# Another order of work at the change of batch, in a layer of attention and routed low-rank adapters on one core

## The chip, the core and the metric

The kernel runs on one core of a Trainium2 chip. Five engines of that core work on their own queues, each strictly in the order in which the program was written: PE (matrix products, with its weight loads PEld shown apart), DVE (vector work), ACT (scalar functions and copies), POOL (further vector work) and SP, which issues all DMAs here. Work on one engine that needs a result of another waits on a semaphore, and everything behind it in its queue waits too. The metric is the device time of one execution in microseconds (us); the page and the trace come from one execution that was profiled.

## What is computed

The input x has 4 batches of 1024 rows with 1024 values each, all in float32. Cut to what matters:

```python
x = x + attention(layernorm(x))       # 32 heads of 32 values, rotary q and k, causal, then @ wo
x = x + ffn(layernorm(x))

# attention, per batch
q, k, v = xn @ wq, xn @ wk, xn @ wv
q, k = rotate(q), rotate(k)
probs = softmax(where(causal, q @ k.T / sqrt(32), lowest))
out = (probs @ v) @ wo

# ffn: one of 8 adapters of rank 16 per row
logits = yn @ route_w.T
best, which = top_k(logits, 1)
h = yn @ A.T                          # 8 x 16 values
out = (one_hot(which) * best * h) @ Bw
```

## The kernel before

*Units.* The four heads of one group fill the 128 partitions. A unit is one batch and one group: 4 batches of 8 groups are 32 units. While the scores, the softmax and the value products of unit u run, PE's free time is filled with the projections of unit u+1, and, from batch 1 on, with the output projection, the second layer norm and the adapter of one block of 128 rows of the batch before. The end of a batch is where this text looks: the first projections of the next batch need its rows normalized and transposed, while the last two units of the old batch are still at their scores.

*Rounds.* The eleven entries of SLOTS (line 26) are the rounds of one unit. A score round writes scores of one or more blocks of 64 rows (numbered 0 to 15; "round 12" below is the one that writes block 12) into PSUM. There is one such PSUM tile (`s`, four banks), which the value products (`av`) use too. ACT copies the scores out (L412), POOL adds the causal mask on the diagonal (L415), DVE finds the maxima (L433) and joins those of the two halves (L454), ACT makes the exponentials (L462), DVE transposes them in 32x32 blocks (L487), and PE multiplies them with the values (L568). "first" and "second" apply the value products of blocks 0 to 7 and 8 to 15. After the value products DVE scales the result by the reciprocal sums (L588), and only then is the PSUM tile free.

*Filling.* What PE does between the rounds is a list of steps, `between[u]`, with a cost each. `do_some` takes steps from the list until a round's share of the costs is used up. A step of cost 0 (a load, a fetch, a scaling) goes with the next one that has a cost. Nothing is planned by time: the order of the lists is the order of the queues.

- `chain(u, n, tb)`: eight matmuls of 128x512 that project q, k or v of unit u for the first or the second half of the rows (tb 0 or 1). After the last, ACT copies the result out; for q and k, DVE and POOL rotate it some steps later (L340 to L346). When the second half of one of q, k, v is done, its weights are free and the next weight load is issued; two weight tiles are in rotation.
- `finish_steps(b, t)`: of one block of rows of the finished batch. `fetch` loads its attention and its x; sixteen output matmuls (`po`, L685) follow, whose weights are streamed in chunks; then the second norm. Its four `tail` steps come in the next unit: `turn` (eight transposes of the normalized rows, `pt_f`; one half is copied out by ACT, the other by DVE, L204), `route` (`ph`, L706, and five small DVE steps to the gated hidden values `wh`, L725), `turn_hidden` (`pw`, one transpose) and `adapt` (`pf`, L745, two matmuls, two DVE additions, and the store).
- `Norm` (line 233): the eight blocks of 128 rows ("tiles" 0 to 7) of the next batch. `load` brings tiles in; some land in the tiles that later hold q and k of the next unit (`homes`), the others in one of five row buffers. `find` makes the moments of one tile (two L175, L177, L179 on DVE, then a power on POOL, L181). `scale` applies them (L186 on DVE); before it scales tile k, it finds the moments of tile k+1. `turn` transposes a scaled tile on PE (`pt_a`, L198, two PSUM banks), has ACT copy it into `xnT` (L200, L202), and loads the tiles that `after` names. There are two `xnT` tiles, one for each half of the rows.

*Where the steps of Norm stand.* `change_steps` (line 783) makes the filling of a batch's last unit: the first eight output matmuls mixed with the tail, with the scaling and turning of tiles 2 and 3 and of tile 4, then the chains of the next unit with turns 4 to 7 among them. The first tiles are put into the list of the unit before, by counting places from its end (lines 819 to 837): for batch 0 turns 0 to 3 stand between the last matmuls of that list; from batch 1 on only turn 0 stands there, and turn 1 comes in `change_steps`.

*Buffers.* Apart from the two weight tiles there are five row buffers, four for q and k, two `xnT`, four chunks, one PSUM tile of four banks for scores or value products and four PSUM banks for everything else.

Of the kernel before, what the change touches and what calls it, by code (L numbers as in the profile page):

```python
# [71 lines left out]
def tile_preln_attn_then_top1_lora(  # L72
# [160 lines left out]
    class Norm:  # L233
# [30 lines left out]
        def scale(self, t):  # L264
            while self.scaled <= t:
                k = self.scaled
                self.find(k + 1)
                normalize(self.x[k], self.x[k], self.moments.pop(k))
                self.scaled += 1

        def turn(self, t):
# [8 lines left out]
            self.load(*self.after.get(t, ()))  # L280

# [501 lines left out]
    def change_steps(u, norm, project, tail):  # L783


        p, turning, scaling = project, norm.turning, norm.scaling
# [3 lines left out]
        if p:  # L790
            turn, route, turn_hidden, adapt = tail
            out += [*p[:2], turn, scaling(2), p[2], turning(1), p[3], route, scaling(3), p[4], turning(2)]
            out += [p[5], turn_hidden, p[6], turning(3), adapt, Step(lambda: norm.load(7), 0.0)]
            out += [scaling(4), p[7]]
            chains = weave(chains[:-6], p[8:]) + chains[-6:]
        else:
            out += [scaling(4)]
        for t, n in zip(range(TB, NT), (3, 4, 5, 4)):
            out += chains[:n] + [turning(t)] + [scaling(t + 1)] * (t + 1 < NT)
            del chains[:n]  # L800
        return out + chains
# [4 lines left out]
    for u, (b, g) in enumerate(units):  # L806
        project, new_tail = [], []
        if b:
# [3 lines left out]
            if g:  # L812
                between[-1].insert(max(0, len(between[-1]) - 8), fetch)
# [5 lines left out]
        if u + 1 < len(units) and g + 1 == NG:  # L819
            last_v = between[-1]  # L820
            if b:
                norm = Norm(b + 1, {0: (1,), 1: (4,), 2: (5,), 3: (6,)}, {2: "q", 3: "k", 5: "q", 6: "k"})
                last_v.append(norm.scaling(1))
                last_v.insert(len(last_v) - 9, norm.turning(0))
                last_v.insert(len(last_v) - 18, norm.scaling(0))
                last_v.insert(len(last_v) - 30, Step(lambda norm=norm: norm.load(0), 0.0))
            else:
                norm = Norm(b + 1, {0: (5,), 1: (6,), 2: (7,)})
                for t in reversed(range(TB)):
                    last_v.insert(len(last_v) - 7 + 2 * t, norm.turning(t))  # L830
                for t in (3, 2):
                    last_v.insert(22 * t - 34, norm.scaling(t))
# [3 lines left out]
            steps = change_steps(u + 1, norm, project, tail)  # L836
            norms[b + 1] = norm
        else:
            steps = []
            if u + 1 < len(units):  # L840
                for n, tb in (("q", 0), ("k", 0), ("q", 1), ("k", 1), ("v", 0), ("v", 1)):
                    steps += chain(u + 1, n, tb)
# [261 lines left out]
```

## Time and profile before

| | us |
|---|---|
| median of 3 runs | 2793.89 (2791.73 to 2795.76) |
| the profiled execution | 2790.88 |
| its span, first to last instruction | 2789.1 |
| PE busy | 2699.2 |
| DVE busy | 2132.6 |
| ACT busy | 1753.3 |
| POOL busy | 646.6 |
| mean granted clock of PE | 0.991 |

Busy time is that of the engine's own instructions, without their waits. The granted clock is the share of full speed that PE was given; in a stretch where it is 0.5, PE is as busy as ever and does half the work. The wait table says for each engine and line who released it, with the sum, the number of waits and the longest. Times in an excerpt in order of time count from the start of the span; a bracket behind an instruction tells how long its engine stood idle before it and who ended that. In counts, one matmul of float32 appears as two records. The batches change at about 515 to 570, 1170 to 1255 and 1865 to 1950 us.

### The profile page before, as it was taken

To read this page: it belongs to the slowest core of one execution; us is meant where nothing else is said; L and a number is where in the kernel's file an instruction comes from. 1 tells how busy PE (TensorE), PEld (TensorE's weight loads), DVE (VectorE), ACT (ScalarE), POOL (GpSimd) and SP (SyncE) were. 2 spreads that over 40 slices of the span, in tenths; PEclk is the share of its full clock that TensorE was granted. 3 is DMA by queue.
4 is the path that set the end of the run, shared out by engine and by line. 5 is a ranking of instruction groups with operands and counts; after the bars stand their busy time and mean duration, and the time that the engine had idled before them with its cause. 6 is when DMAs were issued, how large, how long until landed. Compare 5 with 4: busy or idle time off the path is not lost.

```text
span 2789.1 us, 84093 instructions
## 1 busy us (share of the span) xinstructions
PE 2699.2 (97%) x35328; PEld 1329.6 (48%) x35328; DVE 2132.6 (76%) x4201; ACT 1753.3 (63%) x5030; POOL 646.6 (23%) x900
## 2 busy tenths in 40 slices
PE   8999999899999999979999999997999999999998
PEld 5444444444444554444444455443544445544445
DVE  4888889897777778767777777876777777787655
ACT  2877877776666667546666666664676666666421
POOL 2222233232222222222222222221222222222000
PEclk9999999999999999989999999999999999999999
DMA  3222232226444444541654444454265444346421
GB/s 116 51 55 55 62 97 55 66 55 163 142 123 134 115 124 133 154 140 54 170 141 129 130 120 121 128 162 131 59 167 145 123 135 122 118 124 191 129 66 54
DMA packets 448011, 317.86 MB, mean 114 GB/s; under 512 B 150288, under 2 KB 371728, under 8 KB 447632
## 3 DMA queue, kind: packets, MB, share of 16 engines
q1 hardware_dynamic: 447632, 312.47, 40.3%
q8 instruction: 278, 4.55, 0.7%
q14 instruction: 101, 0.83, 0.1%
HBM read 262.59 MB, written 49.81 MB: 112 GB/s over the span
## 4 chain that ended last, share of the span: by engine, by line
PE 83%; DVE 13%; ACT 2%; POOL 1%; issue 1%; DMA 0%; POOLq 0%; SPq 0%; ACTq 0%; DVEq 0%
PE po L685 15%; PE pk L308 14%; PE pq L308 14%; PE pv L308 12%; PE s L401 11%; PE av L568 9%; DVE top L433 4%; DVE pr L487 4%; PE pf L745 2%; PE ph L706 2%; ACT pr L412 1%; PE pr L542 1%; DVE both L454 1%; PE pt_f L198 1%; PE pt_a L198 1%
## 5 line engine op out<-in xcount | busy, mean ns | idle before, releaser
L462 ACT ACTIVATE pr<-pr,both 128x256 f32<-128x256 f32 (+15 forms) x2048 | 1044.9, 519 | 38.9 <-DVE both L454 38.8
L412 ACT COPY pr<-s 128x640 f32<-128x640 f32 (+14 forms) x544 | 525.1, 1017 | 518.1 <-PE s L401 517.5
L433 DVE TENSOR_REDUCE top<-pr 128x2 f32<-128x960 f32 (+15 forms) x768 | 650.9, 894 | 259.0 <-POOL pr L415 258.6
L487 DVE STREAM_TRANSPOSE pr<-pr 128x1024 f32<-128x1024 f32 (+11 forms) x768 | 664.9, 907 | 42.3 <-ACT pr L462 39.0
L415 POOL TENSOR_TENSOR pr<-pr,causal_sb 128x128 f32<-128x128 f32 x512 | 239.7, 474 | 1108.7 <-ACT pr L412 1100.0
L308 PE MATMUL pv<-xnT,wv 128*128 128x512 f32 x1024 | 485.2, 602 | 0.0
L308 PE MATMUL pq<-xnT,wq 128*128 128x512 f32 x1008 | 478.2, 601 | 0.6 <-ACT xnT L200 0.6
L308 PE MATMUL pk<-xnT,wk 128*128 128x512 f32 x1008 | 475.6, 602 | 0.0
L401 PE MATMUL s<-kT,qT 32*32 32x256 f32 (+4 forms) x17408 | 398.1, 390 | 10.9 <-ACT pr L412 4.2
L462 ACT ACTIVATION_READ_ACCUMULATOR pr<-pr,both 128x1 f32 x2048 | 400.7, 196 | 0.0
L685 PE MATMUL po<-chunk,attn 128*128 128x512 f32 x736 | 378.7, 599 | 0.0
L401 PEld LDWEIGHTS s<-kT,qT 32*32 32x32 f32 x17408 | 188.8, 103 | 268.1 <-issue 101.0
L308 PEld LDWEIGHTS pk<-xnT,wk 128*128 128x128 f32 x1008 | 182.6, 190 | 236.7 <-issue 235.4
L308 PEld LDWEIGHTS pv<-xnT,wv 128*128 128x128 f32 x1024 | 186.5, 190 | 218.1 <-issue 213.8
L308 PEld LDWEIGHTS pq<-xnT,wq 128*128 128x128 f32 x1008 | 182.9, 191 | 224.5 <-issue 222.0
L568 PE MATMUL av<-pr,vals 64*32 64x256 f32 (+3 forms) x12288 | 269.8, 318 | 3.6 <-DVE pr L487 3.5
L568 PEld LDWEIGHTS av<-pr,vals 64*32 64x32 f32 x12288 | 212.1, 105 | 111.4 <-issue 36.0
L454 DVE TENSOR_TENSOR both<-top 32x4 f32<-32x4 f32 (+3 forms) x1152 | 216.3, 188 | 23.5
L685 PEld LDWEIGHTS po<-chunk,attn 128*128 128x128 f32 x736 | 135.0, 191 | 163.8 <-issue 153.6
L543 ACT COPY by<-pr 128x512 f32<-128x512 f32 x64 | 37.4, 585 | 266.8 <-PE pr L542 262.8
L588 DVE TENSOR_TENSOR at<-av,by 128x256 f32<-128x256 f32 x128 | 48.1, 417 | 171.1 <-ACT by L543 171.1
L685 PE MATMUL po<-wo,attn 128*128 128x512 f32 x256 | 118.2, 603 | 0.0
(87 smaller groups left out, 1728.8 us busy)
## 6 DMA issues: line engine op xcount, KB each, us to landing
chunk<-in_wo SPq DMA_DIRECT2D x368, 256.0 KB, 3.4
vals<-vd SPq DMA_DIRECT2D x256, 128.0 KB, 4.1
x<-in_x SPq DMA_DIRECT2D x56, 512.0 KB, 4.8
wq<-in_wq SPq DMA_DIRECT2D x32, 512.0 KB, 4.1
wk<-in_wk SPq DMA_DIRECT2D x32, 512.0 KB, 4.1
wv<-in_wv SPq DMA_DIRECT2D x32, 512.0 KB, 4.2
vd<-vT SPq DMA_DIRECT2D x128, 128.0 KB, 4.6
out_y<-x SPq DMA_DIRECT2D x32, 512.0 KB, 2.8
```

The source lines that it names most:

```text
L198: nc.tensor.transpose(pt[:, i, :], src[:, c * P : (c + 1) * P], eye_sb)
L308: nc.tensor.matmul(at["p"], lhsT=wt[:, c, :], rhs=xnTs[b, tb][:, c, :], start=(c == 0), stop=(c == NC - 1),)
L401: nc.tensor.matmul(sc[i * SQ : (i + 1) * SQ, h, at : at + w].rearrange("p (j k) -> p j k", k=SQ), lhsT=of_q[rows, 2 * t + half], rhs=of_k[ ...
L412: nc.scalar.copy(pr[:, :, k0 : k0 + w], sc[:, :, at : at + w])
L415: nc.gpsimd.tensor_tensor(diagonal, diagonal, causal_sb.unsqueeze(1).to_broadcast([P, HG, SQ]), ALU.add)
L433: nc.vector.tensor_reduce(top[:, k, h : h + step], places[u, t][:, h : h + step, :], AX.X, ALU.max, negate=True,)
L454: nc.vector.tensor_tensor(dst[rows], src[rows], src[other], op)
L462: nc.scalar.activation(pr[:, h, :], pr[:, h, :], AF.Exp, bias=tops[u, t][:, h : h + 1], accum_out=dens[u, t // QT][:, t % QT, h : h + 1],)
L487: nc.vector.transpose(pr, pr)
L568: nc.tensor.matmul(avs[half][h * HD : (h + 1) * HD, t0:, :], lhsT=v[rows, j, h * HD : (h + 1) * HD], rhs=rhs, start=(j == 0), stop=(j == n ...
L685: nc.tensor.matmul(st["po"], lhsT=lhsT, rhs=rhs, start=(c == start), stop=(c == stop))
L706: nc.tensor.matmul(ph, lhsT=st["ynT"][:, c, :], rhs=w[:, c - i * RA, :], start=(c == 0), stop=(c == NC - 1),)
```

## The change

No arithmetic is changed. What is changed is where steps stand in the lists, and which tile of the next batch is loaded where.

1. *Order of the last chains.* The unit after which a batch ends projects in the order q0, q1, k0, v0, k1, v1 (the digit is the half of the rows), where all units had q0, k0, q1, k1, v0, v1. So everything that reads the first half of `xnT` is done two chains earlier.
2. *One chain a unit on.* From batch 1 on, the last of these chains, v1, is left out of that list (`held`) and done in `change_steps` of the next, where it takes the place among the tail that the first eight output matmuls had. Those follow later in the same list.
3. *Moments and scaling as steps of their own.* `finding(t)` is a new step. From batch 2 on (`self.b` of the norm over 1), moments of tile k are found in such steps or just ahead of the scaling, and `scale` no longer finds those of k+1. For the norm of batch 1, `scale` finds k+1 after scaling k instead of before it.
4. *Places.* For the norm of batches 2 and 3 the moments, scalings and turns of tiles 0 and 1 and moments and scaling of tile 2 now stand in the list of the unit before, each behind a named chain step. For that of batch 1, turns 0 to 3 stand from the second matmul of k1 on.
5. *Loads.* From batch 2 on tiles 3 and 4 are put into the q and k tiles and later tile 6 into q's (it was 2, 3, 5 and 6), so one tile more uses a row buffer. The fetch for the last unit of a batch stands 3 places from the end of its list instead of 8.

```diff
         def scale(self, t):
             while self.scaled <= t:
                 k = self.scaled
-                self.find(k + 1)
+                self.find(k + 1 if self.b == 0 else k)
                 normalize(self.x[k], self.x[k], self.moments.pop(k))
                 self.scaled += 1
+                if self.b == 1:
+                    self.find(k + 1)
...
+        def finding(self, t):
+            return Step(lambda: self.find(t), 0.0)
...
-    def change_steps(u, norm, project, tail):
+    def change_steps(u, norm, project, tail, held):
...
         if p:
             turn, route, turn_hidden, adapt = tail
-            out += [*p[:2], turn, scaling(2), p[2], turning(1), p[3], route, scaling(3), p[4], turning(2)]
-            out += [p[5], turn_hidden, p[6], turning(3), adapt, Step(lambda: norm.load(7), 0.0)]
-            out += [scaling(4), p[7]]
+            find = norm.finding
+            out += [*h[:2], turn, *h[2:4], turning(2), h[4], find(3), route, h[5], scaling(3), find(4)]
+            out += [h[6], turn_hidden, h[7], p[0], adapt, Step(lambda: norm.load(7), 0.0), scaling(4)]
+            out += [p[1], find(5), p[2], scaling(5), turning(3), p[3], p[4], turning(4), *p[5:8]]
             chains = weave(chains[:-6], p[8:]) + chains[-6:]
-        else:
-            out += [scaling(4)]
-        for t, n in zip(range(TB, NT), (3, 4, 5, 4)):
-            out += chains[:n] + [turning(t)] + [scaling(t + 1)] * (t + 1 < NT)
-            del chains[:n]
-        return out + chains
+            out += [*chains[:2], find(6), *chains[2:4], scaling(6), turning(5), *chains[4:6], find(7)]
+            out += [*chains[6:8], scaling(7), turning(6), *chains[8:14], turning(7)]
+            return out + chains[14:]
+        out += [*chains[:3], scaling(5), turning(4), *chains[3:7], scaling(6), turning(5)]
+        out += [*chains[7:12], scaling(7), turning(6), *chains[12:16], turning(7)]
+        return out + chains[16:]
+
+    USUAL = (("q", 0), ("k", 0), ("q", 1), ("k", 1), ("v", 0), ("v", 1))
+    ENDING = (("q", 0), ("q", 1), ("k", 0), ("v", 0), ("k", 1), ("v", 1))
+
+    def behind(steps, at, step):
+        steps.insert(steps.index(at) + 1, step)
...
-                between[-1].insert(max(0, len(between[-1]) - 8), fetch)
+                apart = 3 if g + 1 == NG and u + 1 < len(units) else 8
+                between[-1].insert(max(0, len(between[-1]) - apart), fetch)
...
             if b:
-                norm = Norm(b + 1, {0: (1,), 1: (4,), 2: (5,), 3: (6,)}, {2: "q", 3: "k", 5: "q", 6: "k"})
-                last_v.append(norm.scaling(1))
-                last_v.insert(len(last_v) - 9, norm.turning(0))
-                last_v.insert(len(last_v) - 18, norm.scaling(0))
-                last_v.insert(len(last_v) - 30, Step(lambda norm=norm: norm.load(0), 0.0))
+                norm = Norm(b + 1, {0: (2,), 2: (5,), 3: (6,)}, {3: "q", 4: "k", 6: "q"})
+                load = [Step(lambda norm=norm, t=t: norm.load(t), 0.0) for t in range(2)]
+                for at, step in (
+                    (own["k", 0][0], load[0]),
+                    (own["v", 0][0], norm.finding(0)),
+                    (own["v", 0][1], load[1]),
+                    (own["v", 0][2], norm.scaling(0)),
+                    (own["v", 0][6], norm.turning(0)),
+                    (own["v", 0][7], norm.finding(1)),
+                    (own["k", 1][0], norm.scaling(1)),
+                    (own["k", 1][3], norm.turning(1)),
+                    (own["k", 1][5], norm.finding(2)),
+                    (own["k", 1][7], norm.scaling(2)),
+                ):
+                    behind(last_v, at, step)
             else:
                 norm = Norm(b + 1, {0: (5,), 1: (6,), 2: (7,)})
-                for t in reversed(range(TB)):
-                    last_v.insert(len(last_v) - 7 + 2 * t, norm.turning(t))
-                for t in (3, 2):
-                    last_v.insert(22 * t - 34, norm.scaling(t))
+                for t, at in enumerate((("k", 1), ("k", 1), ("k", 1), ("v", 1))):
+                    behind(last_v, own[at][(1 + 3 * t) % NC], norm.turning(t))
+                behind(last_v, own["v", 1][5], norm.scaling(4))
+                behind(last_v, own["k", 0][0], norm.scaling(3))
+                behind(last_v, own["q", 0][6], norm.scaling(2))
...
-            steps = change_steps(u + 1, norm, project, tail)
+            steps = change_steps(u + 1, norm, project, tail, held)
...
+            held = []
             if u + 1 < len(units):
-                for n, tb in (("q", 0), ("k", 0), ("q", 1), ("k", 1), ("v", 0), ("v", 1)):
-                    steps += chain(u + 1, n, tb)
+                ends = g + 2 == NG and b + 1 < B
+                own = {}
+                for n, tb in ENDING if ends else USUAL:
+                    own[n, tb] = chain(u + 1, n, tb)
+                    if ends and b and (n, tb) == ("v", 1):
+                        held = own[n, tb]
+                    else:
+                        steps += own[n, tb]
...
             if b:
-                norms[b + 1].load(2, 3)
+                norms[b + 1].load(3, 4)
```

More of the change, by code (lines that the diff above doesn't have):

```diff
@@ L780, in finish_steps @@
         return Step(fetch, 0.0), chains, tail
-    def change_steps(u, norm, project, tail):
-        p, turning, scaling = project, norm.turning, norm.scaling
+    def change_steps(u, norm, project, tail, held):
+        p, h, turning, scaling = project, held, norm.turning, norm.scaling
         out, chains = [], []
```

## The prediction

> **What bounds the kernel now.** First the page: which engine is full, over the whole span.
>
> ```profile
> PE 2699.2 (97%) x35328; PEld 1329.6 (48%) x35328; DVE 2132.6 (76%) x4201; ACT 1753.3 (63%) x5030; POOL 646.6 (23%) x900
> PEclk9999999999999999989999999999999999999999
> ```
>
> PE does nearly all of the span; an order can win only its 90 us of idle time and the time at half clock. Second, the wait table of PE, for who holds it up:
>
> ```profile
> PE pt_a L198 <- DVE x L186: 22.1, 7, 9.2
> PE pt_a L198 <- DVE kT L186: 19.6, 4, 7.4
> PE ph L706 <- DVE yn L204: 8.5, 3, 3.3
> ```
>
> Columns are total us, times, longest. The transposes of the next batch's rows wait for DVE's scaling (L186), and route waits for a DVE copy. Third, windows around the three changes of batch, and one ordinary stretch after the second:
>
> ```profile
> 502.00:570.00 68.00, 58.14 (x1013) 32.42 (x1028) 57.06 (x111) 49.36 (x133) 16.65 (x24) 0.92 0.21 55
> 1153.00:1253.00 100.00, 79.86 (x1062) 43.85 (x1061) 73.94 (x145) 50.00 (x138) 20.00 (x29) 0.92 0.49 143
> 1847.00:1950.00 103.00, 81.03 (x1062) 42.52 (x1061) 74.02 (x145) 50.56 (x140) 19.51 (x29) 0.93 0.47 138
> 1253.00:1353.00 100.00, 100.00 (x1221) 46.42 (x1220) 73.88 (x150) 66.75 (x189) 28.37 (x36) 0.99 0.37 94
> ```
>
> After the length come PE, PEld, DVE, ACT and POOL busy, then the granted clock. The changes cost 9.9, 20.1 and 22.0 us of idle PE, and clocks of 0.92 to 0.93 (8 to 9% of 58 to 81 busy us: 5 to 7 us each): some 70 us in all, the ceiling of any gain. Fourth, the second change in order of time, PE and then DVE:
>
> ```profile
> 1195.06 2.85 PE L706 MATMUL ph<-chunk,yn 128*128 128x136 f32 x16 [3.25 <-DVE yn L204]
> ...
> 1209.92 1.94 PE L198 MATMUL pt_a<-eye_sb,kT 128*128 128x128 f32 x8 [6.05 <-DVE kT L186]
> ...
> 1230.18 1.06 PE L198 MATMUL pt_a<-eye_sb,qT 128*128 128x128 f32 x8 [1.37 <-DVE qT L186]
> ...
> 1240.65 1.94 PE L198 MATMUL pt_a<-eye_sb,kT 128*128 128x128 f32 x8 [3.07 <-DVE kT L186]
> ...
> 1251.06 1.94 PE L198 MATMUL pt_a<-eye_sb,x 128*128 128x128 f32 x8 [3.07 <-DVE x L186]
> ```
>
> ```profile
> 1198.30 0.81 DVE L186 TENSOR_SCALAR qT<-qT,mv_a,rstd_a 128x1024 f32<-128x1024 f32 x1
> ...
> 1199.99 0.29 DVE L725 TENSOR_TENSOR wh<-ph,gate 128x128 f32<-128x128 f32 x1
> 1200.20 3.24 DVE L487 STREAM_TRANSPOSE pr<-pr 128x704 f32<-128x704 f32 x4
> ...
> 1204.37 2.21 DVE L433 TENSOR_REDUCE top<-pr 128x4 f32<-128x768 f32 x3
> ...
> 1207.33 1.29 DVE L175 BATCH_NORM_STATS2 st_a<-x 128x6 f32<-128x512 f32 x2
> ...
> 1208.97 0.81 DVE L186 TENSOR_SCALAR kT<-kT,mv_a,rstd_a 128x1024 f32<-128x1024 f32 x1
> ```
>
> DVE works from 1177 to 1209.8 with no break but three of 0.7 for POOL, while PE stands; then it stands while PE catches up. So the question at each change is when DVE's queue, in its new order, reaches what PE next needs.
>
> **The change, part by part.** No operation is added or taken away: the built queues of both hold the same instructions, in another order. One full-width matmul takes 0.857 us of PE, a turn (eight transposes) 0.88.
>
> *Second change.* PE. Up to round 12 of the last unit but one, PE has 26 matmuls of the unit's chains and 12 of the output projection behind it where it had 30 and 11: 3 fewer, 2.6 us, so round 12 starts at 1150.9 instead of 1153.43 (no new wait: DVE still stood 7 us between 1126 and 1154). From round 12 to the hidden transpose (pw) the new queue holds 25 full-width matmuls (21.4), five score rounds (0.92+1.43+1.43+1.37+1.57=6.7), the value chain of block 0 with its transpose (2.8), four turns (3.5) and route (1.9): 36.4 us. Alone, PE would be there at 1187.3.
>
> DVE. Its first link is the maximum of round 13, which ends at 1153.1 (1155.4 before, less the rotation of q, 1.4, now done earlier, and 0.9 for PE being ahead by one matmul). From there to the gate (wh), durations from its rows: both halves 0.7, rotation of k 1.45, moments of tile 0 1.63, transposes of 1024 columns 2.31, scaling 0.87 (7.0); attention scaling 0.7, transposes 4.14, maxima of 12 2.62, moments 1.63, maxima of 11 2.51, scaling of tile 1 0.73 (12.3); FFN moments and scaling 3.9; transposes 1.89, maxima of 10 3.69, moments and scaling of tile 2 with 0.67 for POOL between them (8.8); rotation of k's second half 1.45, transposes 1.75, maxima of 7 2.9, copy of yn 0.73 (6.8); transposes 3.26, reciprocals 0.95, maxima of 5 2.96, moments of tile 3 1.63, gate 1.26 (10.1). Sum 48.9: wh at 1202.0. PE must wait 14.7 us before it, about 2.6 at turn 1, 2.7 at turn 2, 3 to 3.5 at route and 6 at pw. **The waits move forward; they don't all go.** Rotation of k (second half) and the long transposes, which stood elsewhere, now stand ahead of the gate.
>
> After pw the gain comes. PE has 25 full-width matmuls (21.4, the adapter's two among them), the two value pieces (6.4), rounds 2, 15 and 14 (4.0) and five turns (4.4): 36.4 with pw, to 1238.4. Tiles 3, 4, 5 are scaled by 1204, 1211 and 1214, turned at 1212, 1217 and 1226. Tile 6 is scaled 8.0 after round 2 ends (before: maxima end 4.2 after, halves 0.7, moments 1.6, POOL 0.7, scaling 0.8) and turned after 8.0 of PE's work; tile 7 takes 7.0 against 8.0. The waits of 6.05, 1.37, 3.07 and 3.07 go. Turn 7 ends at 1238.4 with 2 matmuls fewer done than before at 1252.0: 11.9 us gained, with half clock after 1252 1.5 more (before's window reaches to 1255), less 2.1 for half clock after the new wait at pw: 11.3.
>
> *Third change*: the same queues; before took 102.0 us for the stretch that took 98.6, so 13.2 (3.4 more, and no 1.5 behind it).
>
> *First change*: scaling of tiles 3 and 4's moments, and a rotation, are out of DVE's way before round 13, so the maxima of 13 start at about 506 (511.86 before). Then halves and transposes to 511, attention scaling when PE has come that far (515.2), transposes 4.14, maxima and rotation 2.62+1.45+2.5+1.89+3.69, scaling of tile 4 at 532.2 (PE waits 3.0), moments, transposes, maxima, scaling of tile 5 at 539.2 (1.1), moments and last transposes 544.1, which the value chain needs (4.0). From there PE has 17.8 us to the end of turn 7: 561.9 instead of 569.7. Less 1.7 of half clock: 6.
>
> Loads: the eight row loads a batch, two weight loads and fetches only change places on SP's one queue. Row 1 of the new order waits for ACT's copy of an older tile, done long before; the fetch of y waits for turn 1 (1174) and rows 5 for turn 2 (1187); behind the latter stand the adapter chunks, needed at 1204 and landing in 3.4. wk is now loaded at 1203, needed at 1232. Nothing there sets the end; a chunk of the three output matmuls in a row may be late by 0.3 to 0.8 (the row "PEld po <- DMA chunk" knows 0.8).
>
> Two rules of the Trainium skill speak here. **Contention**: these rows are the same operation, alone and beside POOL's cosine product.
>
> ```profile
> 1159.18 0.70 DVE L342 TENSOR_TENSOR swapk<-swapk,sin_sb 128x512 f32<-128x512 f32 x1
> 1241.18 1.52 DVE L342 TENSOR_TENSOR swapq<-swapq,sin_sb 128x512 f32<-128x512 f32 x1
> ```
>
> "GPSIMD Engine Reference", Specifications, says that GpSimd shares its SBUF interfaces with DVE, to the cost of DVE instructions with two SBUF inputs. The second rotation of k now stands in the full stretch: 0.8 us later per change, 1.6 for two. **Clock**: "TensorE: Matmul & The Clock Gate", Why this matters, asks for no idle gaps over about 3 us. By it only the wait at pw costs clock. Here a wait of 2.21 at 1868 was followed by a clock of 0.62 over 1869.5 to 1873, so I charge the shorter ones also; those before pw cost nothing while DVE sets the pace. By the page alone the sum would be 1.7 better.
>
> Off for contention 1.6, late chunks 1, and 0.14 us between the end of a scaling and PE's start, 15 times, 2.1. Sum: 11.3+13.2+6-4.7=25.8. The profiled execution took 2790.9, so 2765.1; the median of runs lies 3.0 above it: **2768 us**.
>
> **Rivals.**
> A (0.62), as above: waits move forward, about 40 of 70 us remain. With DVE's first link 2 us earlier or later at each change and one 3 us wait too many or too few: 2758 to 2780.
> B (0.15): DVE comes in time, since its order ahead of pw is less tight than my sum (an idle half-clock round, or ACT ahead). For it: DVE is busy only 74 of 100 us. Against: the 48.9 us have no gap that I can find. Waits at pw and route gone: 2 x 9.5 and 7 for the first change more, 2742.
> C (0.13): little changes. Each new wait ahead of pw also delays ACT's copies and so the next maxima, and DVE idles 7 us per change: 2788.
> D (0.10), slower: ACT runs in order, and a turn's two copies stand in it ahead of exponentials that DVE's long transposes need. I find 2.7 us of slack there. If a copy comes late by more than that plus the gain of some 8.5 per change, 11 us, the loss begins; at 15 late in each of three, 2804. For it: DVE's transposes waited 4.05 for such exponentials at 546; against: ACT is busy 50 of 100 us.
>
> **Numbers.** A measurement tells 0.2%, 5.6 us, from no change. Faster: A, B and half of C, 0.84; same: the rest of C, 0.06; slower: D, 0.10. B's lower end and D's upper lie outside the range: 2746 to 2790.
>
> **What would show it.** Right: waits at ph and pw of 3 and 6 us at the second and third change, none at turns 4 to 7, turn 3 no longer waiting. Wrong: no wait at pw (B), or DVE idle before pw on ACT's exponentials (C, D).

## The result, and the profile after

The changed kernel takes 2775.1 us (median of 6 runs, 2773.19 to 2776.26), the kernel before 2793.38 beside it on the same chip: a ratio of 0.9935, with a 95% interval of 0.9925 to 0.9945. The profiled execution's span went from 2789.1 to 2773.1 us. The forecast was 2768, range 2746 to 2790, and rival A's own range 2758 to 2780: the time lies in both, the gain is 16 us of span instead of 25.8.

The page of the changed kernel, first its engine row and the granted clock:

```profile
PE 2695.8 (97%) x35328; PEld 1328.7 (48%) x35328; DVE 2133.2 (77%) x4201; ACT 1754.4 (63%) x5030; POOL 637.7 (23%) x900
PEclk9999999999999999999999999999999999999999
```

PE is busy 3.4 us less for the same matmuls (it runs a little less at half clock), and the gain is 12.6 us of idle time besides. Its wait table (total us, times, longest):

```profile
PE pt_a L198 <- DVE x L186: 23.9, 8, 9.5
PE ph L711 <- DVE yn L204: 9.3, 3, 3.6
PE pw L740 <- DVE wh L730: 9.0, 2, 4.5
PE av L573 <- DVE pr L492: 5.8, 3, 2.9
```

The 19.6 us of turns that waited for a tile in the k buffer are gone, and pw, where nothing had waited, now waits 4.5 at two changes. The windows of after (length, busy PE, PEld, DVE, ACT, POOL, then the clock), the three changes and an ordinary stretch:

```profile
500.00:570.00 70.00, 58.97 (x999) 31.85 (x998) 57.11 (x116) 53.15 (x147) 15.86 (x26) 0.98 0.21 55
1150.00:1250.00 100.00, 84.99 (x1106) 44.68 (x1105) 79.76 (x159) 57.96 (x164) 21.03 (x33) 0.95 0.49 144
1840.00:1940.00 100.00, 86.67 (x1108) 46.04 (x1109) 81.12 (x161) 58.32 (x161) 20.21 (x32) 0.95 0.46 137
1250.00:1350.00 100.00, 100.00 (x1194) 47.19 (x1193) 74.80 (x151) 64.79 (x179) 28.09 (x36) 1.00 0.37 97
```

At the second and third change 15 and 13 us of PE are idle where 20 and 22 were in the forecast's windows (the third of those is 3 us longer). At the first it is 11.0 where 9.9 were. The second change in order of time on PE:

```profile
1174.66 1.10 PE L198 MATMUL pt_a<-eye_sb,x 128*128 128x128 f32 x8 [2.65 <-DVE x L186]
...
1188.27 1.06 PE L198 MATMUL pt_a<-eye_sb,x 128*128 128x128 f32 x8 [3.20 <-DVE x L186]
...
1195.40 2.80 PE L711 MATMUL ph<-chunk,yn 128*128 128x136 f32 x16 [3.63 <-DVE yn L204]
...
1205.41 0.45 PE L740 MATMUL pw<-eye_sb,wh 128*128 128x128 f32 x1 [4.49 <-DVE wh L730]
...
1216.94 1.04 PE L198 MATMUL pt_a<-eye_sb,qT 128*128 128x128 f32 x8
...
1240.18 2.84 PE L313 MATMUL pk<-xnT,wk 128*128 128x512 f32 x6 [1.00 <-ACT xnT L200]
...
1245.79 1.04 PE L198 MATMUL pt_a<-eye_sb,x 128*128 128x128 f32 x8
```

Three waits stand ahead of pw and a fourth at it, none at turns 3 to 7. And the ends of DVE's queue that set them, with the two places where it lost time:

```profile
1152.17 2.08 DVE L438 TENSOR_REDUCE top<-pr 128x2 f32<-128x896 f32 x2 [1.19 <-POOL pr L420]
...
1171.26 1.81 DVE L438 TENSOR_REDUCE top<-pr 128x2 f32<-128x768 f32 x2 [1.09 <-POOL pr L420]
...
1186.37 1.75 DVE L186 TENSOR_SCALAR x<-x,mv_a,rstd_a 128x1024 f32<-128x1024 f32 x1 [0.73 <-POOL rstd_a L181]
...
1204.97 0.29 DVE L730 TENSOR_TENSOR wh<-ph,gate 128x128 f32<-128x128 f32 x1
```

*Where the 16 us come from.* Each unit has one score round of 512 columns, so its start marks equal progress in any of the kernels. Between such starts of the profiled executions, in us:

| stretch | before | after | difference | forecast |
|---|---|---|---|---|
| up to there | 417.18 | 417.20 | +0.02 | 0 |
| first change (417.18 to 643.72 before) | 226.54 | 227.52 | +0.98 | -6 |
| to the second | 407.36 | 407.36 | 0 | 0 |
| second change (1051.08 to 1415.51) | 364.43 | 357.33 | -7.10 | -11.3 |
| to the third | 329.37 | 329.43 | +0.06 | 0 |
| third change (1744.88 to 2110.79) | 365.91 | 356.10 | -9.81 | -13.2 |
| rest | 678.31 | 678.16 | -0.15 | 0 |
| sum | 2789.1 | 2773.1 | -16.0 | -30.5, +4.7 off = -25.8 |

The ordinary stretches agree to 0.1 us. Two things make a stretch longer than its work: PE's idle time, and what half clock takes (half of PE's busy time there). At the second change the idle time went from 20.1 to 15.3 and the loss by half clock from 6.8 to 4.2; at the third from 22.0 to 13.3 and from 5.6 to 5.1; at the first from 14.4 up to 15.3 and from 6.2 to 4.6, and PE's own work there came out 1.7 longer, for which no cause was looked for. The question that was left: why is the first change worth nothing?

### The profile page after: what moved, and what is told of

It reads as the page before. It is cut to its first block, busy times and chain, and to the rows that moved or that the text cites. A ratio compares the mean times of both kernels' runs of the same rounds, so it can differ in the third digit from the quotient of the medians.

```text
span 2773.1 us, 84079 instructions
## 1 busy us (share of the span) xinstructions
PE 2695.8 (97%) x35328; PEld 1328.7 (48%) x35328; DVE 2133.2 (77%) x4201; ACT 1754.4 (63%) x5030; POOL 637.7 (23%) x900
## 4 chain that ended last, share of the span: by engine, by line
PE 81%; DVE 14%; ACT 2%; POOL 1%; issue 1%; DMA 0%; SPq 0%; POOLq 0%; ACTq 0%; DVEq 0%
PE po L690 15%; PE pq L313 14%; PE pk L313 13%; PE pv L313 12%; PE s L406 11%; PE av L573 9%; DVE top L438 4%; DVE pr L492 4%; PE pf L750 2%; PE ph L711 2%; DVE both L459 1%; PE pr L547 1%; PE pt_f L198 1%; ACT pr L417 1%; ACT pr L467 1%
## 5 line engine op out<-in xcount | busy, mean ns | idle before, releaser
L420 POOL TENSOR_TENSOR pr<-pr,causal_sb 128x128 f32<-128x128 f32 x512 | 238.7, 473 | 1077.1 <-ACT pr L417 1068.3
```

Of the source, the lines that this page charges most:

```text
L420: nc.gpsimd.tensor_tensor(diagonal, diagonal, causal_sb.unsqueeze(1).to_broadcast([P, HG, SQ]), ALU.add)
```

## The experiments

All carry the new order unless they say otherwise. A table at the end of this section has every run by the same stretches.

### The change in two halves

In one kernel the lists of batch 0's end are new and the others old, in the other the reverse.

```diff
-                ends = g + 2 == NG and b + 1 < B
+                ends = g + 2 == NG and b == 0            # the first alone
+                ends = g + 2 == NG and 0 < b < B - 1     # the others alone
...
```

(and with it the `Norm` lines, the body of `change_steps` and the finding in `scale` of the batches concerned.)

> The new order at the first change of batch alone; the second and third as before. Theory now (the gain is made at the second and third change alone, because at the first one the mask of the round of 96 columns waits on POOL behind the moments of tile 4 and takes back what DVE saved): 2793 to 2796, no gain, a loss of up to 1.5. Rival (the prediction's sum, first change worth 6): 2787.

> The new order at the second and third change alone; the first as before. Theory: all of the gain or a little more, 2773 to 2775. Rival (first change worth 6): 2781. In both the waits at the gate's transpose stay 4.5 and those at route 3.6.

Measured: the first alone 2795.66 against 2795.55 beside it, ratio 1.0002 (0.9994 to 1.001); the others alone 2775.86, ratio 0.9928 (0.9915 to 0.994). So the new order of the first change gives nothing, and the forecast's 6 us for it are refuted; the second and third give all of it. The single parts of the new order at a change (chains, places, loads) were not tried one by one, but for the chain a unit on, below. The waits in the second kernel are those of after (pw 4.6 and 4.7, route 3.6).

### What held the first change back

The forecast said that with scalings and a rotation out of DVE's way "the maxima of 13 start at about 506 (511.86 before)". Here are DVE's maxima at three points of the first change, before:

```profile
488.56 2.78 DVE L433 TENSOR_REDUCE top<-pr 128x4 f32<-128x384 f32 x5 [1.86 <-POOL pr L415]
...
511.86 2.08 DVE L433 TENSOR_REDUCE top<-pr 128x2 f32<-128x896 f32 x2 [1.19 <-POOL pr L415]
...
524.34 1.81 DVE L433 TENSOR_REDUCE top<-pr 128x2 f32<-128x768 f32 x2
```

and in the changed kernel:

```profile
493.54 2.79 DVE L438 TENSOR_REDUCE top<-pr 128x4 f32<-128x384 f32 x5 [2.32 <-POOL pr L420]
...
511.12 2.08 DVE L438 TENSOR_REDUCE top<-pr 128x2 f32<-128x896 f32 x2 [1.19 <-POOL pr L420]
...
529.98 1.81 DVE L438 TENSOR_REDUCE top<-pr 128x2 f32<-128x768 f32 x2 [1.86 <-POOL pr L420]
```

The first of them is 5.0 late, the last 5.6; between the first and the second DVE gained the 5.7 that were forecast, from a start that was too late. The first and the last wait 2.32 and 1.86 for a mask on POOL (L420). POOL's queue of the changed kernel says what stood ahead of those masks:

```profile
491.30 0.55 POOL L181 TENSOR_TENSOR rstd_a<-ve_a,half_sb 128x1 f32<-128x1 f32 x1 [4.22 <-DVE ve_a L179]
491.82 1.28 POOL L351 TENSOR_TENSOR qT<-qT,swapq 128x512 f32<-128x512 f32 x1
493.05 2.12 POOL L420 TENSOR_TENSOR pr<-pr,causal_sb 128x128 f32<-128x128 f32 x5
...
528.27 1.27 POOL L351 TENSOR_TENSOR kT<-kT,swapk 128x512 f32<-128x512 f32 x1 [9.29 <-DVE swapk L347]
529.50 0.45 POOL L420 TENSOR_TENSOR pr<-pr,causal_sb 128x128 f32<-128x128 f32 x1
```

The scaling of tile 3 with the moments of tile 4 behind it was put ahead of that round on DVE. Their power (L181) was so put ahead of the masks on POOL, and waits 4.22 us for DVE to come to it; DVE, once done with the moments, waits 2.32 for its own mask. The second pair is the last k chain: since it now ends just before the round, the sum of its rotation stands ahead of the mask and waits for DVE. Two kernels move the moments of tile 4 (taken from behind the scaling of tile 3 in both):

```diff
-                if self.b == 1:
+                if self.b == 1 and k != 3:
                     self.find(k + 1)
...
+                behind(last_v, own["k", 1][7], norm.finding(4))   # the first
+                behind(last_v, own["k", 1][5], norm.finding(4))   # the second
```

> The changed kernel, with the moments of tile 4 at the first change taken from behind the scaling of tile 3 and put behind the last matmul of the second k chain, past the masks of two rounds. Theory (POOL's queue holds the mask back): the maxima of the round of 96 columns start at about 490.7 instead of 493.5, DVE waits under 1 us for that mask instead of 2.32, and the first change gets 2 to 3 us shorter: 2772 to 2773.5. Rival (PE's own rounds and ACT set that stretch): the mask comes earlier and the time stays 2775.

> The changed kernel with the moments of tile 4 at the first change put after the sixth matmul of the second k chain, into DVE's wait for the copy of the turned sums. Theory (with the earlier run: POOL holds back first the mask of the round of 96 columns, then that of the round of 384, which stands behind the sum of the rotated k): DVE comes to the maxima of 768 at about 527.8 instead of 529.98, turn 4 waits under 1.5 instead of 3.0 and the value chain under 1.5 instead of 2.9: 2771 to 2773. Rival (PE's rounds and ACT set the stretch): within 1 us of the changed kernel.

The first of the two, DVE again:

```profile
491.26 2.79 DVE L438 TENSOR_REDUCE top<-pr 128x4 f32<-128x384 f32 x5 [1.57 <-POOL pr L420]
...
508.82 2.08 DVE L438 TENSOR_REDUCE top<-pr 128x2 f32<-128x896 f32 x2 [1.20 <-POOL pr L420]
...
530.30 1.81 DVE L438 TENSOR_REDUCE top<-pr 128x2 f32<-128x768 f32 x2 [1.86 <-POOL pr L420]
```

The mask came earlier, as the theory says (though 1.57 us were still waited for it, not under 1), and DVE was 2.3 ahead up to the maxima of 896. So 2.3 of the 5.0 us were the power's. Another 1.2 PE had lost before: its round of 96 columns starts at 485.84 instead of 484.61, behind a longer wait at 443 (3.44 instead of 2.81) and a longer half clock (6.8 us instead of 3.4). The remaining 1.5 were not tried. Then the moved moments stood at 524.31, ahead of the rotation of k, and at the second mask all of it was lost: first change 227.39, no gain, 2777.5 us: the rival's outcome, but not for its reason. So the second mask is a second obstacle. The second kernel puts the moments where DVE waits for ACT anyway. Its DVE and PE:

```profile
528.48 1.81 DVE L438 TENSOR_REDUCE top<-pr 128x2 f32<-128x768 f32 x2 [1.86 <-POOL pr L420]
```

```profile
537.81 1.97 PE L198 MATMUL pt_a<-eye_sb,x 128*128 128x128 f32 x8 [2.95 <-DVE x L186]
...
548.82 4.22 PE L573 MATMUL av<-pr,vals 64*32 64x256 f32 x128 [1.27 <-ACT xnT L200]
```

DVE is there 1.5 earlier than in the changed kernel (2.2 were expected), turn 4 still waits 2.95 (under 1.5 expected), the value chain 1.3 instead of 2.9, turn 5 and the sums' transpose no longer. The stretch took 223.47 instead of 227.52: 4.05 gained, 3.4 of it idle time of PE. The clock has no part in it: half clock lasted 10.2 us in both, 3.4 less after the wait at 443 and 3.4 more around turn 4 and the value chain. So the first change then is 3.1 better than before, half of the forecast's 6. In the run's time: 2774.49, ratio 0.9925 (0.9913 to 0.9937), not told apart from the changed kernel's, since its other two changes were 0.6 and 1.2 worse. So POOL's order is shown to have cost the first mask 2.3 us. The sum of k still stands ahead of the second mask (1.86 waited); that without it the 6 us would be had was not tried.

### Does DVE's queue set the wait at pw?

```diff
-            ... h[4], find(3), route, h[5], scaling(3), find(4)]
+            ... h[4], route, h[5], find(3), scaling(3), find(4)]      # moments of tile 3 behind the gate
```

```diff
-            transposed(st["ynT"], st["yn"], f"f{name}", scalar_only=at_end)
+            transposed(st["ynT"], st["yn"], f"f{name}", scalar_only=at_end or t == NG - 2)   # yn by ACT
```

> The changed kernel with the moments of tile 3 at the second and third change behind the gate on DVE instead of ahead of it, nothing else. Theory (DVE's queue sets the gate one for one): the gate ends 1.6 us earlier, the wait at the hidden transpose is 2.9 instead of 4.5 at both changes, and the time 2 to 3.5 lower, 2771 to 2773. Rival (another wait takes it up: turn 3 or the adapter): the wait falls, the time stays within 1 us.

> The changed kernel with the second half of the turned yn copied by ACT instead of DVE at the second and third change (0.7 us less on DVE, one copy more on ACT). Theory (waits move along PE's queue, their sum is set by DVE at the hidden transpose): the wait of 3.6 at route goes, that at the hidden transpose grows from 4.5 to about 7.4, the time falls by 0.7 a change, 2773 to 2774.5. Rival (the waits stand each for itself): the wait at the hidden transpose stays 4.5 and the time falls by 7, 2768.

PE at pw of the second change, in the first of the two and then in the second:

```profile
1202.23 0.30 PE L740 MATMUL pw<-eye_sb,wh 128*128 128x128 f32 x1 [2.93 <-DVE wh L730]
```

```profile
1205.82 0.45 PE L740 MATMUL pw<-eye_sb,wh 128*128 128x128 f32 x1 [9.14 <-DVE wh L730]
```

With the moments behind the gate the time from the start of the maxima of 896 to the gate's last step falls from 52.80 to 51.19, the 1.6 us of the moments, and the wait from 4.49 to 2.93 (third change 4.49 to 3.13). The run took 2769.57, ratio 0.9911 (0.9897 to 0.9924), a little better than expected; the second change took 353.2 instead of 357.3 (idle time 3.2 less, loss by half clock 0.8 less), the third only 0.65 less. With ACT's copy the wait at route is gone and pw waits 9.14 and 7.09: the waits are one sum that DVE sets, and the rival that each stands for itself is out. Its 2772.85 (ratio 0.992, 0.9908 to 0.9933) is just under what the theory expected. That 9.14 is more than the 7.4 expected has a reason in the rows: with no wait at route, route and the matmuls behind it run at full clock and PE is at pw earlier still. At its third change the gate came 1.0 later instead of 0.7 earlier: DVE waited there 1.48 for ACT's copy of the sums (0.17 in the changed kernel) and 0.60 for exponentials.

### Turning later

If DVE sets pw, PE should have more to do ahead of it. The first kernel puts turn 1 three, turn 2 four and route seven matmuls on and the hidden transpose behind the value chain, with output-projection matmuls between.

```diff
-                    (own["k", 1][3], norm.turning(1)),
                     (own["k", 1][5], norm.finding(2)),
+                    (own["k", 1][6], norm.turning(1)),
...
-            out += [*h[:2], turn, *h[2:4], turning(2), h[4], find(3), route, h[5], scaling(3), find(4)]
-            out += [h[6], turn_hidden, h[7], p[0], adapt, ...]
+            out += [*h[:2], turn, p[0], h[2], p[1], h[3], p[2], h[4], turning(2), find(3), p[3], *h[5:8]]
+            out += [route, p[4], scaling(3), p[5], find(4), p[6], scaling(4), p[7], turn_hidden, p[8]]
+            out += [adapt, ..., find(5), scaling(5), p[9], turning(3)]
...
```

> The changed kernel, with PE's steps at the second and third change put later against DVE's queue: turn 1 three matmuls on, turn 2 four, route seven, the hidden transpose behind the value chain; output-projection matmuls fill the places. Theory (DVE's 51 us set the hidden transpose, and PE stands because it comes 14 us too early): idle PE before the hidden transpose falls from 14.0 to under 5 us a change, no new wait over 2.5 behind it, 2752 to 2760. Rival (the work taken from behind is missed there: turns 3 to 7 wait instead): 2770 to 2778.

In this kernel the rotated q is written over tile 6 before it is turned, so that other values than tile 6's are turned; up to turn 5 its queue is the one meant. It took 2792.26, as long as the kernel before (ratio 0.999). Its PE at turn 2:

```profile
1187.51 0.63 PE L198 MATMUL pt_a<-eye_sb,x 128*128 128x128 f32 x4 [0.58 <-DVE x L186]
1194.37 1.12 PE L198 MATMUL pt_a<-eye_sb,x 128*128 128x128 f32 x4 [6.23 <-DVE yn L204]
```

The first half is turned at once, and the second waits 6.23 for a PSUM bank: with an output chain and a value chain open there are four banks for them, both halves of turn 2 and the half of the turned yn that DVE has not yet copied out. The bank is counted from the tiles that are open; the row names only DVE's copy. Pw itself waited for nothing. Behind it turn 6 waited 6.65 for the rotation, the fault named above, and turn 7 5.23 for DVE's scaling. So the rival's mechanism was right for this kernel, new waits took the place, though its 2770 to 2778 left out the one at turn 2. The next one is mended:

```diff
+            k0, q0, rest = chain(u, "k", 0), chain(u, "q", 0), []     # k ahead of q: tile 6 lies in q's buffer
...
+            out += [*k0[:3], turning(4), *k0[3:6], turning(5), find(6), *k0[6:], p[10], scaling(6)]
+            out += [*q0[:2], find(7), p[11], *q0[2:4], turning(6), scaling(7), p[12], *q0[4:7]]
+            out += [turning(7), q0[7], p[13]]
...
+            transposed(..., scalar_only=at_end or t == NG - 2)        # the bank of yn comes free by ACT
```

> As the run before it of the same kind (turn 1, turn 2, route and the hidden transpose later on PE, output-projection matmuls in their places), mended where that one stood: ACT alone copies the turned yn, so that its PSUM bank comes free without DVE; the k chain of block 0 goes ahead of the q chain, so that tile 6 is turned before the rotated q is written over it; tiles 6 and 7 are found and scaled before the round of 480 columns. Theory (DVE's 50 us from the maxima of 896 to the gate set the hidden transpose, PE's 36 us of work before it are too few): idle PE under 5 us in all at each of the two changes, 2752 to 2760. Rival (a PSUM bank, a row load or the scaling of tile 7 takes the place): one new wait of 5 us or more at each change, 2767 to 2775.

All its waits of over 0.5 us on PE at the second change:

```profile
1189.18 1.07 PE L198 MATMUL pt_a<-eye_sb,x 128*128 128x128 f32 x8 [0.58 <-DVE x L186]
...
1196.96 3.75 PE L711 MATMUL ph<-chunk,yn 128*128 128x136 f32 x16 [3.28 <-ACT xnT L200]
...
1212.94 1.98 PE L750 MATMUL pf<-chunk,whT 128*128 128x512 f32 x4 [1.14 <-ACT whT L742]
...
1237.82 1.64 PE L198 MATMUL pt_a<-eye_sb,qT 128*128 128x128 f32 x8 [2.38 <-DVE qT L186]
```

2760.69, ratio 0.9878 (0.9863 to 0.9893), just above what the theory expected. Pw waits no more, though the gate comes at 1204.88 as in the changed kernel (1204.97): DVE's queue need not be shortened when PE has other work to do. Some 8 us a change stay idle, more than the 5 expected, the largest part (3.28) for ACT's copies of turn 2, which stand behind exponentials; route needs their bank, as it seems. The last two kernels put route ahead of turn 2, the moments of tile 3 behind the gate and those of tile 6 ahead of turn 5, take in the second kernel of the first change, and (the second only) leave tile 1's moments for later in batch 0:

```diff
+            route.cost = 0.5                                          # one or two more steps ahead of the value product
-            ... h[4], turning(2), find(3), p[3], *h[5:8]]
-            out += [route, p[4], ...
+            ... h[4], p[3], *h[5:8], route, turn2, p[4]]              # turn2: turning(2) at no cost
+            out += [find(3), scaling(3), p[5], find(4), p[6], scaling(4), turn_hidden, ...
...
-                if self.b == 1 and k != 3:
+                if self.b == 1 and k not in (0, 3):                   # the second only
```

> The version with everything later, with three more steps: route ahead of turn 2 on PE (a bank for it is free before ACT has copied turn 2), the moments of tile 3 behind the gate, those of tile 6 ahead of turn 5, and at the first change the moments of tile 4 behind the sixth matmul of the second k chain. Theory: at the second and third change the idle PE falls from 8 to under 6 us, at the first change by 3: 2750 to 2756. Rival (the waits only move to the first value chain, which needs DVE's transposes of 288): one wait of 5 us there, and only the first change's 3 us come in, 2756 to 2759.

> The run before, and in batch 0 the moments of tile 1 of the next batch not behind the scaling of tile 0 but just ahead of the scaling of tile 1. Theory (POOL's rstd of tile 1 holds up the mask of the round of 512 columns, and with it all maxima up to the PE wait of 3.4 at 443): that wait falls to 2.5 or less and a half-clock stretch goes: 1.5 to 4 us below the run before. Rival (DVE's 1.6 us and the wait for POOL stand 30 us later, where PE also waits for DVE): within 1 us of the run before.

The windows of the first:

```profile
500.00:570.00 70.00, 63.36 (x1070) 33.90 (x1069) 60.05 (x122) 54.73 (x152) 16.39 (x27) 0.95 0.23 61
1150.00:1250.00 100.00, 92.11 (x1189) 46.42 (x1187) 84.63 (x172) 63.57 (x176) 23.18 (x36) 0.98 0.52 148
1840.00:1940.00 100.00, 92.01 (x1152) 46.42 (x1151) 79.91 (x161) 62.63 (x172) 23.52 (x34) 0.98 0.47 138
```

2753.58, ratio 0.9852 (0.9838 to 0.9865): more than twice the gain of the change that was studied, from the same instructions but for a few copies that ACT makes instead of DVE. 8 us a change are still idle (7.9 in the second window), so "under 6" was missed; the longest, 3.63, is the second half of turn 2, which waits for ACT's copy of the second value chain (for its bank, as it seems; the trace names the engine, not the bank). In the second kernel the wait at 443 fell from 3.5 to 1.3 and its half clock went, as the theory said, and waits for ACT and DVE behind it took all of it back: 2753.46, the rival's outcome.

### The chain a unit on

```diff
-                    if ends and b and (n, tb) == ("v", 1):
-                        held = own[n, tb]
-                    else:
-                        steps += own[n, tb]
+                    steps += own[n, tb]
...
+            h, p = p[:8], p[8:]
```

(and the fetch 8 places from the end again.)

> The changed kernel without the one chain a unit on: at the second and third change the second value chain is done in its own unit, and eight output-projection matmuls stand where its eight did; all else in the new order. Theory (what counts is how many full-width matmuls stand between the maxima of 896 columns and the hidden transpose, not which): pw waits 4 to 6 us as with the chain, and the time is within 3 us of the changed kernel, 2773 to 2780. Rival (the chain held back is what covers DVE's queue): without it 7 us more are idle at each of two changes, 2787 to 2792.

2781.31, ratio 0.995 (0.9937 to 0.9964): between the two. The second change took 361.2, the third 360.0, 3.9 worse each. Its longest waits of PE up to pw, at turn 0, turn 2 and pw:

```profile
1160.53 1.97 PE L198 MATMUL pt_a<-eye_sb,x 128*128 128x128 f32 x8 [3.82 <-DVE x L186]
...
1199.69 1.11 PE L198 MATMUL pt_a<-eye_sb,x 128*128 128x128 f32 x4 [3.39 <-ACT yn L200]
...
1215.18 0.45 PE L740 MATMUL pw<-eye_sb,wh 128*128 128x128 f32 x1 [5.97 <-DVE wh L730]
```

So neither "it does not matter which matmuls stand there" nor "7 us a change" holds. Of the gain at the two changes, 16.9 us, the chain a unit on makes some 8 and the order of the other steps the rest. But the run changes more than which matmuls stand at the tail. With eight steps more in the list, turn 0 comes ahead of the value product of blocks 0 to 7 instead of behind it, and waits 3.82 where it had waited for nothing, with 6.8 us at half clock in that place (1158.77 to 1165.60, none in the changed kernel); of the 3.9 us at the second change 2.6 are half clock and 1.3 idle time, at the third 0.6 and 3.0. What is due to turn 0 alone was not tried. That an output chain beside the tail holds a bank where a finished value chain does not would fit the second row, but was not tried by itself.

### All runs by stretch

| kernel | first | second | third | rest | median | ratio to before |
|---|---|---|---|---|---|---|
| before | 226.5 | 364.4 | 365.9 | 678.3 | 2793.4 | |
| after | 227.5 | 357.3 | 356.1 | 678.2 | 2775.1 | 0.9935 |
| first change alone | 226.3 | 367.2 | 366.3 | 678.2 | 2795.7 | 1.0002 |
| second and third alone | 226.8 | 357.0 | 356.1 | 681.8 | 2775.9 | 0.9928 |
| moments of tile 4 late | 227.4 | 357.5 | 355.9 | 681.5 | 2777.5 | 0.9936 |
| moments of tile 4 before the sums | 223.5 | 357.9 | 357.3 | 678.1 | 2774.5 | 0.9925 |
| moments of tile 3 behind the gate | 225.9 | 353.2 | 355.5 | 678.4 | 2769.6 | 0.9911 |
| yn by ACT | 227.9 | 357.5 | 358.3 | 676.1 | 2772.9 | 0.9920 |
| turns later, first | 227.3 | 364.3 | 365.9 | 681.5 | 2792.3 | 0.9990 |
| turns later, mended | 228.1 | 349.5 | 349.3 | 676.0 | 2760.7 | 0.9878 |
| the same and the first change | 223.6 | 348.8 | 347.4 | 674.6 | 2753.6 | 0.9852 |
| the same, tile 1's moments late | 225.7 | 347.6 | 348.7 | 674.4 | 2753.5 | 0.9850 |
| v1 not a unit on | 228.1 | 361.2 | 360.0 | 676.6 | 2781.3 | 0.9950 |

The medians come from several jobs, in which the kernel before took 2793.4 to 2795.8; each ratio is against the kernel before in its own job. The stretches are of one execution each: where the order is the same as in before or after, they differ by up to 2.7 us at the second change (364.4 and 367.2) and by up to 5.2 in the rest.

## Why the prediction was right, and where it was not

*Waits move forward (rival A).* Right, place by place. Forecast were waits of 2.6 at turn 1, 2.7 at turn 2, 3 to 3.5 at route and 6 at pw, 14.7 in all; the second change shows 2.65, 3.20, 3.63 and 4.49, 13.97 in all, the third 2.65, 1.51, 3.63 and 4.49, and none at turns 3 to 7. At the third the wait at turn 1 was followed by 3.4 us at half clock, and the next wait is 1.7 shorter: ahead of pw, what the clock takes comes off the next wait. Rival B (no wait at pw) is out. Rival C is out as put: between the maxima and the gate DVE stood for POOL (1.09, 0.67 and 0.73), not for ACT's exponentials. D did not come at the second and third change; something of its kind is seen at the first, where the copies of turns 0 to 3 stand among ACT's exponentials and DVE waited 2.75 for ACT's copy of the sums.

*DVE's sum to the gate, 48.9.* (Of the three breaks that the forecast saw in DVE's work before, two were for POOL, at 1179.98 and 1188.80; the third, 0.56 at 1177.00, was for PE. The sum does not rest on it.) Measured 51.0 (1154.25 to 1205.26): right but for 2.1. The wait of 1.09 for a mask was not in the sum, and the scaling of tile 2 took 1.75 instead of 0.8. The first link, end of the maxima of 896, was forecast at 1153.1 and came at 1154.25, of which 1.0 is what the first change lost.

*PE's 36.4 to pw.* Measured 53.4 from round 12 (1152.02) to pw (1205.41), less 14.0 of waits: 39.4. Of the 3 us more some 1.8 are half clock behind the wait at route: ph took 2.80 in this place and 2.02 at 1121.84 in the same trace, the two matmuls behind it 2.93 instead of 1.88. The rest is the starts, as in the next point. They cost nothing, as the forecast said of what lies ahead of pw: the wait at pw is by so much shorter.

*PE's 36.4 from pw to the end of turn 7.* Measured 41.3 (to 1246.7). 2.6 of it is half clock (2.1 were charged for it), 1.0 a wait for ACT's copy of turn 6 that the sum had not, and the rest the starts: a matmul beside a round or a turn took 0.95 to 0.97 where 0.857 was counted, some ten times. Together with DVE's 2.1 this is why the second change gave 7.1 and not 11.3, the third 9.8 and not 13.2: the terms were each too small by some us, the mechanism was the one described.

*The first change, 6.* Here a step failed: "scaling of tiles 3 and 4's moments, and a rotation, are out of DVE's way before round 13, so the maxima of 13 start at about 506". They started at 511.12. What was taken from DVE there had been put ahead of an earlier round, and with it a power on POOL ahead of that round's masks; the 5 us were lost at 493 already, 2.3 of them to that power and 1.2 to PE's own delay. The forecast took the start of that earlier round as given and asked of DVE's queue alone, though the trace of before showed all four maxima between 488 and 512 waiting for POOL (1.05 to 1.86). The sum from there on was right: 39.7 measured from the maxima to the last transposes, 38.1 forecast; turn 4 waited 2.95 (3.0), turn 5 0.72 (1.1), the value chain 2.9 (4.0).

*Off 4.7.* Contention: 1.6 were charged for the second rotation of k beside POOL's cosine product. The rotation came behind the product and took its 0.69; the scaling of tile 2 stood beside it instead, 1.75 for 0.81, twice in the kernel: 1.9 in all, the size right, the instruction wrong. Late chunks, 1: no chunk was waited for at the changes. The 2.1 for starts behind a scaling can't be told apart: turns 3 to 7 did not wait.

*Loads.* Right: no wait for a row, a weight or a fetch.

*The clock.* The Trainium skill, "TensorE: Matmul & The Clock Gate", Why this matters, warns of gaps over about 3 us. In the changed kernel half clock goes with the waits of 3.63 at route and 4.49 at pw, as the page has it, but not with the 3.20 at turn 2; and it does go with 2.65 at turn 1 of the third change. The forecast's charge for shorter waits does not sort these either: the length of a wait does not tell, its place does. In each of the thirteen traces all stretches at half clock start whole multiples of 3.413 us apart, and last one, two or three such pieces. Windows of the changed kernel cut at these places:

```profile
1183.03:1186.44 3.41, 2.04 (x7) 0.73 (x5) 2.50 (x10) 2.45 (x8) 0.65 (x2) 1.00 0.61 243
1186.44:1189.85 3.41, 1.58 (x10) 1.12 (x10) 3.38 (x5) 1.86 (x6) 1.34 (x2) 1.00 0.00 0
...
1193.27:1196.68 3.41, 1.28 (x11) 1.28 (x12) 3.22 (x8) 3.41 (x13) 0.91 (x2) 1.00 0.00 0
1196.68:1200.09 3.41, 3.41 (x11) 2.33 (x10) 3.25 (x9) 0.12 (x2) 0.48 (x1) 0.50 0.60 198
1200.09:1203.51 3.42, 0.83 (x2) 0.00 (x0) 3.31 (x9) 0.00 (x0) 0.13 (x1) 1.00 0.09 35
1203.51:1206.92 3.41, 1.51 (x3) 0.94 (x4) 3.20 (x11) 0.27 (x1) 0.55 (x1) 0.50 0.00 0
...
1858.87:1862.28 3.41, 0.76 (x13) 0.65 (x7) 3.30 (x9) 3.12 (x6) 0.00 (x0) 1.00 0.32 95
1862.28:1865.69 3.41, 3.41 (x9) 1.86 (x7) 2.68 (x6) 2.37 (x6) 1.81 (x3) 0.50 0.44 125
```

PE's idle time in a piece is the length less the first busy figure. The wait of 3.20 falls into two pieces, which are idle for 1.37 and 1.83, and the clock stays; the pieces that are idle for 2.13, 2.59 and 2.65 are each followed by half clock. So it is in all thirteen traces, from 150 us to shortly before the end: of 9819 pieces at full clock, each of the 112 with 1.99 us or more idle was followed by half clock, 7 of the 57 between 1.5 and 1.99, and none below. Half clock went on behind each piece in it with over 0.6 us idle and ended behind each with under 0.5. This is read from the traces; no run moved a wait to try it.

## What to carry to other kernels

When an order is changed, follow what each step issues on every engine, the small ones too: here a power of 128 values put ahead of a mask on POOL took back 2.3 of the 5 us by which DVE came late. A wait for an engine that is full over a stretch can't be removed by moving it; count the work that the waiting engine has up to that point, and bring other work there, with its PSUM banks counted, which gave more (2753.6) than the change itself (2775.1).

## What the runs showed of the hardware that was not expected

The scaling, which reads one tensor, is slowed by POOL as the rotation is, which reads two: 1.75 instead of 0.81 us when it starts 0.06 after POOL's cosine product (1186.37 and 1186.31, and again at the third change), but only 0.93 beside two of POOL's masks of 128 columns (yn's scaling at 1177.49, the masks at 1177.42). The Trainium skill, "GPSIMD Engine Reference", Specifications, names beside two SBUF inputs also DVE instructions in a two-port mode; that the scaling is one no run here shows, but the forecast had used only the part on two inputs.

The rest behind the third change has the same order in before, after and several of the kernels, and took 676.6 (v1 not a unit on) to 681.8. The granted clock tells most of these apart: between 2530 and 2600 it is 0.98 in the changed kernel and 0.95 in the kernel with the second and third change alone, for the same waits of 2.0 and 0.8 at route. By how these fall into the pieces of 3.413 us, one of them is followed by 3.4 or by 6.8 us at half clock, which costs 1.7 or 3.4.
